# Window attention on 128 and 64 channels, with values projected once per pixel by way of DRAM

## The chip, the cores and the metric

The kernel runs on one core of a Trainium2 chip. TensorE (PE, with its weight loads as PEld), VectorE (DVE), ScalarE (ACT), GpSimd (POOL) and SyncE (SP) each work through their own list of instructions and meet at semaphores; DMAs are issued from SP and POOL. The metric is the device time of one execution in microseconds. Traces give every instruction its start and length, and the clock that TensorE was granted (1.00 is full speed).

## The reference

Input x is (4, 192, 64, 64) in float32: four images. Four layers follow each other: layer 0 (deformable convolution, attention over channels, MLP), layer 1 (attention of all 4096 pixels with each other), layer 2 (attention in overlapping windows, a high-frequency gate, a gated MLP), and layer 3 (a masked depthwise convolution whose taps depend on the image). The change lies in the first half of layer 2:

```python
y = _conv1x1(_ln_c(x, n1g, n1b), qkv_w, qkv_b)          # norm over 192 channels, then 576 outputs
cols = _unfold(y, WS, STRIDE, PAD)                      # windows of 8x8, every 6 pixels, padded by 3: 11x11
...
attn = jnp.einsum('blhic,blhjc->blhij', q, k)           # 6 heads of 32 channels, 64x64 scores per window
attn = attn + bias[None, None]
e = jnp.exp(attn - jnp.max(attn, axis=-1, keepdims=True))
s = jnp.sum(e, axis=-1, keepdims=True)
s_img = _reverse(s, H, W)                               # sums, folded back and added where windows overlap
o = jnp.einsum('blhij,blhjc->blhic', e, v)
o_img = _reverse(o, H, W).reshape(B, HEADS, ch, H, W)
out = (o_img / s_img[:, :, None]).reshape(B, C, H, W)
```

The padding is of y, so a window's q, k and v are zero outside the image, its scores there are the bias alone, and these enter the sums.

## The kernel before

The images run one after the other. `windows()` does the part above for one image, between layer 1 and `rest()`. It goes through 11 rows of windows (wr = 0..10); a row has three groups of four windows (g = 0..2, the last with three), a group two pairs. Everything inside is written in a fixed order by hand (`tc.manual_schedule()`, the loop from L1330 on), and each engine runs its instructions in that order.

**Layout.** The 192 channels lie as two halves of 96 partitions. A row of windows needs 8 rows of 64 pixels, of which the two upper ones are shared with the row before. `load` (L1077) brings the six new ones from DRAM with one DMA into xr; `norm_steps` (L1107) squares them on ACT (sq, L1112), takes means over the channels on PE (pv, L383), forms the reciprocal root on ACT and DVE (r, L400 to L402, L363, L364), spreads it back over the channels on PE (pb, L392) and multiplies on DVE into the padded tile xs (L1122). `shared` (L1131) copies the two shared rows of xs, qs and ks on POOL. xs has a 97th partition of ones, which carries the bias of the projection.

**Projections.** `project_rows` (L1142) makes q and k of the new rows, for each half two matmul pairs (L1150, L1151) of 384 columns, and ACT writes them to qs (L1154, with the temperature) and ks (L1156). [...]

**Scores.** `scores` (L1176): 24 matmuls of 32 channels for a group (L1185) into the only score tile s (three PSUM banks), then DVE adds the bias (L1191), takes the maximum (L1197) and subtracts it (L1198). `exponentials` (L1201): ACT's exp (L1203), then DVE's sums eh (L1205) and es (L1209).

**Outputs.** `turned` (L1216) projects the values of a pair of windows straight from xw (L1225, two matmuls with 128 pixels out and 192 channels), which ACT copies to vs (L1230), turns the exponentials by three transposes (L1233) and copies them into padded tiles et (L1237). `outputs` (L1243) multiplies values with exponentials (L1253) and adds up the sums per pixel (L1261) into the row's PSUM tile o. `collect` (L1266) copies o to ot (L1271, L1272), POOL adds the overlap with the row before (L1277); `inverses` (L1286) and `finish` (L1295: rb L1298, oi L1299) divide.

**Order.** Group n's transposes and outputs run while the scores of group n + 1 are brought to exponentials; outputs lag one pair behind. In group 0 `project_rows` for the next row stands in both pairs; in group 1 the next x is loaded, the row before is inverted and the norm for two rows on goes as far as its root; in group 2 that norm ends and the row before is finished. Once, after row 1, `load_image` (L2022) loads the whole image for `rest()` with 16 DMAs from SP. PSUM gives s three banks, o two, the norm one, and two banks take turns ("a") for projections, values, transposes and rb.

Of the kernel before, what the change touches and what calls it, by code (L numbers as in the profile page):

```python
# [10 lines left out]
F32 = mybir.dt.float32  # L11
# [58 lines left out]
_WIDE = ["l0_bfc2", "l2_projb", "l2_hftw", "l2_hftb", "l2_fc2b", "l3_bias", "l3_b2"]  # L70
# [11 lines left out]
def conv_seq_kernel(ctx: ExitStack, tc: tile.TileContext, a, out: bass.AP):  # L82
# [86 lines left out]
    for i in range(3):  # L169
# [4 lines left out]
        thetaT, phiT, gT, wW, qkvT, bias, v48, headsel, fc1_dram, fc1_bias, fc1b_dram, fc1b_bias, outb,  # L174
    ) = (None for _ in range(13))
# [10 lines left out]
    def constants():  # L186

        nonlocal thetaT, phiT, gT, wW, qkvT, bias, v48, headsel, fc1_dram, fc1_bias, fc1b_dram, fc1b_bias, outb
# [13 lines left out]
        qkvT = const([P + 1, 2, 3 * C], "qkvT")  # L202
        in_turn(nc.sync.dma_start(out=qkvT[:P], in_=a["qkvT"].rearrange("(k p) n -> p k n", p=P)))
        in_turn(nc.sync.dma_start(out=qkvT[P : P + 1, 1, :], in_=a["qkvb"]))
# [56 lines left out]
        with pool_of(name="foldq", bufs=1, space=PSUM) as pp:  # L261
            p = pp.tile([128, 2, 512], F32, tag="p", name="p_qkv")
            n = 3 * C // 2
            for u in range(2):
                for k in range(2):
                    nc.tensor.matmul(
                        p[P : P + 1, u, 0:n], lhsT=V["l2_n1b"][:, k], rhs=qkvT[:P, k, bass.ts(u, n)], start=k == 0, stop=k == 1
                    )
            row = qkvT[P : P + 1, 1, :].rearrange("p (u n) -> p u n", u=2)
            nc.vector.tensor_tensor(row, row, p[P : P + 1, :, 0:n], ALU.add)  # L270
            for k in range(2):
                nc.vector.tensor_scalar_mul(qkvT[:P, k, :], qkvT[:P, k, :], V["l2_n1g"][:, k])
            centred(qkvT[:P], pp)
# [72 lines left out]
    x_flat = [dram.tile([C, HW], F32, tag=f"xd{i}", name=f"xd{i}") for i in range(2)]  # L346
    xn_drams, x_drams = ([t.rearrange("(k p) n -> p k n", p=P) for t in ts] for ts in (xn_flat, x_flat))
# [712 lines left out]
    def windows(b, oi, load_image):  # L1060
# [3 lines left out]
        with ExitStack() as s:  # L1064
# [4 lines left out]
            given, norms, xws, qws = {}, {}, {}, {}  # L1069

            def new_rows(wr):

                top = STRIDE * wr - PAD
                r0, r1 = (PAD if wr == 0 else WS - STRIDE), min(WS, H - top)
                return r0, r1, top + r0

            def load(wr, by=nc.sync):  # L1077
                r0, r1, at = new_rows(wr)
                t = given[wr] = sb.tile([P, 2, 512], F32, tag="xr", name=f"xr_{b}_{wr}")[:, :, 0 : (r1 - r0) * W]
                by.dma_start(out=t, in_=x_drams[b % 2][:, :, at * W : (at + r1 - r0) * W])  # L1080
# [6 lines left out]
            for j in range(2):  # L1087
                xs = s1.tile([P + 1, 2, WS, SW], F32, tag=f"xs{j}", name=f"xs{j}_{b}")
                qs = s1.tile([P, 2, WS, SW], F32, tag=f"qs{j}", name=f"qs{j}_{b}")
                ks = s1.tile([P, 2, WS, SW], F32, tag=f"ks{j}", name=f"ks{j}_{b}")  # L1090
                for t in (xs, qs, ks):
                    nc.gpsimd.memset(t, 0.0)

                nc.gpsimd.memset(xs[P : P + 1, 1, (PAD if j == 0 else 0) : WS, inside], 1.0)
                sets.append((xs, qs, ks))
            ets = []
            for j in range(3):
                et = s1.tile([128, 3, 2, WS, WS + STRIDE], F32, tag=f"et{j}", name=f"et{j}_{b}")
                nc.gpsimd.memset(et, 0.0)
                ets.append(et)  # L1100
            rss = []
# [5 lines left out]
            def norm_steps(wr, src, dst, rows):  # L1107

                n, name = src.shape[2], f"l2n1_{b}_{wr}"
                q = n // 4  # L1110
                sq = s1.tile([P, 2, 512], F32, tag="ln_sq", name=f"sq_{name}", bufs=2)[:, :, :n]
                nc.scalar.activation(sq, src, AF.Square)  # L1112
                yield SQUARE
                pv = ps.tile([128, 512], F32, tag="n", name=f"pv_{name}")
                variances(pv[:, 0:q], src, mean192)
                variances(pv[:, 128 : 128 + q], sq, mean192)
                r = s1.tile([128, 128], F32, tag="ln_r", name=f"r_{name}", bufs=2)[:, 0:q]
                spread_variance(r, pv[:, 0:q], pv[:, 128 : 128 + q])
                yield from inverse_root_steps(r, r)
                pb = spread_quarters(r, n, P, ps, name).rearrange("p (r c) -> p r c", r=rows)  # L1120
                for k in range(2):
                    nc.vector.tensor_tensor(dst[:, k], src[:, k, :].rearrange("p (r c) -> p r c", r=rows), pb, ALU.mult)  # L1122

            def norm(wr, upto=None):

                r0, r1, _ = new_rows(wr)
                if wr not in norms:
                    norms[wr] = norm_steps(wr, given.pop(wr), sets[wr % 2][0][:P, :, r0:r1, inside], r1 - r0)
                links(norms[wr], upto)

            def shared(wr, i):  # L1131

                to, of = sets[wr % 2][i], sets[1 - wr % 2][i]
                r1 = new_rows(wr)[1]
                if i == 0 and wr == 2:
                    nc.gpsimd.memset(to[P : P + 1, 1, PAD - 1 : PAD, inside], 1.0)
                if wr > 0:
                    nc.gpsimd.tensor_copy(to[:, :, 0 : WS - STRIDE, :], of[:, :, STRIDE:WS, :])
                if r1 < WS:
                    nc.gpsimd.memset(to[:, :, r1:WS, :], 0.0)  # L1140

            def project_rows(wr, h):  # L1142
# [967 lines left out]
```

## Time and profile before

| | |
|---|---|
| median of three runs | 6396.97 us (6394.30, 6396.97, 6414.32) |
| the profiled execution's own time | 6392.29 us |
| its span (first to last instruction) | 6390.5 us |
| window stage of the four images | 268.7, 269.8, 269.0, 271.0 us |
| PE busy in these stretches | 246.7, 247.3, 246.5, 247.3 us |
| a steady row of windows | 23.05 us |
| mean granted clock over the span | 0.963 |

The page of the profile gives for the span the busy time of each engine; then the span in 40 slices; the DMA queues; the chain of work that ended last, by engine and by line; the costliest groups of instructions, with the mean length of one, the idle time of the engine before them and what ended it (its releaser); and the DMA issues. The same can be asked of the trace for a stretch of time, a line or a tile. PE's busy time is that of overlapping matmuls, so their pace is read from start to start rather than from the length of one.

### The profile page before, as it was taken

Reading aid. Unit: us, or ns where it says so; the run is one execution under the profiler, and the core shown is the slowest. Engines: PE = TensorE matmul, PEld = TensorE weight load, DVE = VectorE, ACT = ScalarE, POOL = GpSimd, SP = SyncE. Lnnn points to the kernel's source line nnn. Section 1 sums busy time; section 2 is a strip of 40 time slices with the busy share of each in tenths; the row PEclk is TensorE's granted clock in tenths of the full one; section 3 lists DMA queues with packets and bytes.
Section 4 is the critical chain, followed back from the end, with each engine's and each line's share of the span. In section 5 each row is a group of like instructions: output and inputs, shape, how many; then the busy total and the mean of one; then the engine's idle time right before and its main releaser. Section 6 shows DMA issues by size and latency. Waiting matters only on the chain.

```text
span 6390.5 us, 106371 instructions
## 1 busy us (share of the span) xinstructions
PE 5900.9 (92%) x40528; PEld 4039.0 (63%) x40528; DVE 4612.9 (72%) x6850; ACT 3779.2 (59%) x6552; POOL 2111.3 (33%) x2293
## 2 busy tenths in 40 slices
PE   7888999999989899999988899999998989999897
PEld 4455588886544568887654458888654457776543
DVE  3864199985677669996676839998567867765667
ACT  3764388875654358885654438887565536545542
POOL 2763077752200047772210017775220000003200
PEclk8989999999989999999999999999998999999998
DMA  6995267751010267772110057775111010001000
GB/s 193 308 316 152 81 195 223 224 178 37 24 29 17 74 200 221 226 222 69 35 36 24 21 145 227 222 223 171 36 27 29 21 57 11 13 15 38 5 7 22
DMA packets 330117, 698.60 MB, mean 109 GB/s; under 512 B 59894, under 2 KB 216838, under 8 KB 328839
## 3 DMA queue, kind: packets, MB, share of 16 engines
q0 software_dynamic: 92736, 455.22, 22.0%
q1 hardware_dynamic: 236038, 235.78, 13.5%
q8 instruction: 321, 5.26, 0.3%
q14 instruction: 190, 1.55, 0.1%
q10 hardware_dynamic: 832, 0.79, 0.0%
HBM read 611.25 MB, written 78.87 MB: 108 GB/s over the span
## 4 chain that ended last, share of the span: by engine, by line
PE 63%; DVE 20%; ACT 5%; DMA 5%; issue 4%; SPq 2%; POOL 1%; POOLq 0%; DVEq 0%; ACTq 0%
PE y L1041 11%; PE s L973 10%; PE h L650 7%; DVE ha L1403 2%; PE h L1595 2%; PE qk L1150 2%; PE v L1225 2%; PE o L878 2%; PE qk L1151 2%; DMA ring<-table,idx 2%; DVE ga L1403 2%; PE po L538 2%; DVE gate L1403 2%; DVE row L639 1%; DVE top L980 1%
## 5 line engine op out<-in xcount | busy, mean ns | idle before, releaser
L632 POOL DMA_INDIRECT ring<-table,idx x1152 | 1671.1, 1451 | 946.0 <-DVE row L639 172.7
L973 PE MATMUL s<-ths,ph 96*128 96x256 f32 x4096 | 982.5, 381 | 6.4 <-ACT sc L975 4.0
L973 PEld LDWEIGHTS s<-ths,ph 96*128 96x128 f32 x4096 | 776.6, 191 | 131.1 <-ACT sc L975 6.3
L638 ACT ACTIVATE row<-ring,pos 128x384 f32<-128x384 f32 x1152 | 673.0, 609 | 240.4 <-DVE xo L643 147.2
L639 DVE SCALAR_TENSOR_TENSOR row<-ring,fr,row 128x384 f32<-128x384 f32 x1152 | 673.1, 611 | 111.2 <-ACT row L638 106.3
L1041 PE MATMUL y<-sc,gx 128*97 128x256 f32 x3008 | 716.4, 379 | 0.0
L1041 PEld LDWEIGHTS y<-sc,gx 128*97 128x97 f32 x3008 | 489.3, 164 | 127.5 <-issue 5.1
L642 ACT ACTIVATE xo<-row,pos 128x192 f32<-128x192 f32 x1152 | 485.5, 448 | 64.2 <-PE h L650 32.2
L643 DVE SCALAR_TENSOR_TENSOR xo<-row,fr,xo 128x192 f32<-128x192 f32 x1152 | 445.4, 411 | 41.5 <-ACT xo L642 39.3
L975 ACT COPY sc<-s 128x1024 f32<-128x1024 f32 x376 | 377.1, 1003 | 157.0 <-PE s L973 154.2
L1038 DVE TENSOR_TENSOR sc<-sc,mbs 128x1024 f32<-128x1024 f32 x376 | 453.0, 1217 | 19.8 <-ACT mbs L999 19.7
L1039 ACT ACTIVATE sc<-sc 128x1024 f32<-128x1024 f32 x376 | 393.3, 1053 | 75.2 <-DVE sc L1038 72.1
L980 DVE TENSOR_TENSOR top<-top,sc 128x1024 f32<-128x1024 f32 x282 | 344.0, 1220 | 128.6 <-ACT sc L975 128.4
L650 PE MATMUL h<-ti,xo 128*128 128x192 f32 x2304 | 434.6, 327 | 0.0
L650 PEld LDWEIGHTS h<-ti,xo 128*128 128x128 f32 x2304 | 388.8, 190 | 28.8 <-issue 8.2
L1205 DVE TENSOR_REDUCE eh<-ex 128x12 f32<-128x768 f32 x132 | 125.4, 950 | 317.1 <-ACT ex L1203 317.1
L1403 DVE SCALAR_TENSOR_TENSOR ga<-gate,v,ga 128x1024 f32<-128x1024 f32 x234 | 300.3, 1283 | 6.7
L650 PE MATMUL h<-kept,xo 128*128 128x192 f32 x960 | 239.2, 381 | 70.5 <-DVE xo L643 62.0
L1645 POOL COPY gate<-gate 128x192 f32<-128x192 f32 x12 | 4.2, 348 | 904.9 <-ACT gate L1638 904.9
L650 PEld LDWEIGHTS h<-kept,xo 128*128 128x128 f32 x960 | 169.7, 210 | 162.9 <-DVE xo L643 116.4
L855 PE MATMUL h<-d_l0m,fc 128*128 128x256 f32 x768 | 217.5, 427 | 59.1 <-ACT z L1601 22.5
L1041 PE MATMUL y<-se,gx 128*97 128x256 f32 x1088 | 261.1, 380 | 0.5 <-ACT yn L1047 0.5
(402 smaller groups left out, 11090.8 us busy)
## 6 DMA issues: line engine op xcount, KB each, us to landing
ti<-table SPq DMA_DIRECT2D x768, 48.0 KB
ring<-table,idx POOLq DMA_INDIRECT x1152
xnd<-xn SPq DMA_DIRECT2D x4, 3270.0 KB
xi<-in_x_dram SPq DMA_DIRECT2D x32, 384.0 KB
xk<-xd SPq DMA_DIRECT2D x32, 384.0 KB
xd<-xc SPq DMA_DIRECT2D x64, 192.0 KB
table<-tt SPq DMA_DIRECT2D x32, 384.0 KB
xc<-xd SPq DMA_DIRECT2D x60, 192.0 KB
```

Source lines behind the costliest of these rows:

```text
L632: nc.gpsimd.indirect_dma_start(out=gt.rearrange("p q r c -> p (q r c)"), out_offset=None, in_=corners, in_offset=bass.IndirectOffsetOnAxis ...
L638: nc.scalar.activation(row, gt[:, 0], AF.Copy, scale=pos[:, t, 9 + tap : 10 + tap])
L639: nc.vector.scalar_tensor_tensor(row, gt[:, 1], fr[:, t, 9 + tap : 10 + tap], row, ALU.mult, ALU.add)
L642: nc.scalar.activation(xo[:, j, :], row[:, 0, :], AF.Copy, scale=pos[:, t, tap : tap + 1])
L643: nc.vector.scalar_tensor_tensor(xo[:, j, :], row[:, 1, :], fr[:, t, tap : tap + 1], xo[:, j, :], ALU.mult, ALU.add)
L650: nc.tensor.matmul(acc[m // 2][:, bass.ts(m % 2, C)], lhsT=xo.rearrange("p j c -> p (j c)")[:, bass.ts(m, 128)], rhs=tt, start=t == 0 and ...
L973: nc.tensor.matmul(p[:, t, :], lhsT=ph[:, bass.ts(G * g + t, 128)], rhs=ths[i], start=True, stop=True)
L980: nc.vector.tensor_tensor(tops[i], tops[i], to, ALU.max)
L1038: nc.vector.tensor_tensor(ex, ex, mbs[i].unsqueeze(1).to_broadcast([128, G, QN]), ALU.add)
L1039: nc.scalar.activation(ex, ex, AF.Exp)
L1041: nc.tensor.matmul(py, lhsT=gx[:, G * g + t, :], rhs=ex[:, t, :], start=g == 0 and t == 0, stop=g == NG - 1 and t == G - 1,)
L1403: nc.vector.scalar_tensor_tensor(acc[:, b], src(tap, b), w[:, tap : tap + 1], acc[:, b], ALU.mult, ALU.add)
```

## The change

Channels lie as 128 and 64 partitions (`M`, `Q`) instead of twice 96. Every row of windows takes a strip of six new rows (384 pixels, the last one fewer); the normed strip goes to its own tile xz without padding, and there is no ones row: biases of q and k come as a column (qkb) in ACT's eviction, the bias of the values (vb) in a DVE add. The six projection halves of 96 channels become three tiles of 128: t = 0 (q), t = 1 (k), t = 2 (the last 64 of both).

Values are computed once per pixel, three tiles of 128 pixels per row, written by two DMAs to a DRAM tensor with zero margins (zeroed once, by POOL's DMAs in image 0), and read back window by window by 16 DMAs (8 partitions each) into vw; xw, its POOL copies and the per-pair value matmuls are gone. Each group has one extra matmul of 384 columns (`keep_warm`) ahead of its first transposes. The order of the loop changes with it: t = 0 and t = 2 and the values in group 0, t = 1 in group 1; the sums of the exponentials behind the next group's bias, maximum and subtraction behind the sums (in group 0 behind the first values); the squares of the norm at the end of group 2.

In `constants()`, qkvT is folded with gamma and beta from raw tiles of 128 and 64 rows: the product of the raw weights with beta, which the ones row took before, goes into qkb and vb by ten small matmul groups, a matmul that spreads vb over 128 partitions, and some ten DVE instructions; it is loaded with three DMAs instead of two.

```diff
+            def strip(wr):
+                return (STRIDE if wr < NWIN - 1 else H - STRIDE * wr) * W, STRIDE * wr * W
+            def split(t, n):
+                return t[:, 0, 0:n], t[0:Q, 1, 0:n]
             def load(wr, by=nc.sync):
...
-                by.dma_start(out=t, in_=x_drams[b % 2][:, :, at * W : (at + r1 - r0) * W])
+                by.dma_start(out=lo, in_=x_flat[b % 2][0:M, at : at + n])
+                by.dma_start(out=hi, in_=x_flat[b % 2][M:C, at : at + n])
...
+            def project_rows(wr, t):
+                qs, ks = sets[wr % 2]
+                n = strip(wr)[0]
+                rows, chans = slice(PAD, PAD + n // W), bass.ts(t, M)
+                p = ps2.tile([128, 512], F32, tag="a", name=f"qk_{b}_{wr}_{t}")[:, :n]
+                for k, part in enumerate(split(xzs[wr], n)):
+                    nc.tensor.matmul(p, lhsT=qkvT[0 : part.shape[0], k, chans], rhs=part, start=k == 0, stop=k == 1)
...
+            def values(wr, part):
...
+                tiles = [i for i in (2 * part, 2 * part + 1) if 128 * i < n]
...
+                            nc.tensor.matmul(
+                                p[:, j, :], lhsT=of[:, bass.ts(i, 128)], rhs=qkvT[0 : of.shape[0], k, 2 * C :],
+                                start=k == 0, stop=k == 1,
+                            )
+                    nc.vector.tensor_tensor(
+                        vs[:, tiles[0] : tiles[-1] + 1, :], p, vb.unsqueeze(1).to_broadcast([128, len(tiles), C]), ALU.add
+                    )
+                if part == 0:
+                    return
...
+                for h in range(2):
+                    nc.sync.dma_start(out=to[h], in_=vs[half(h), 0:m, :])
+            def fetch(wr):
+                vw = vws[wr] = sb.tile([128, (NWIN + 1) // 2, C], F32, tag="vw", name=f"vw_{b}_{wr}")
+                for i in range(2):
+                    n = (NWIN + 1 - i) // 2
+                    for r in range(WS):
+                        row = values_dram[STRIDE * wr + r, STRIDE * i : STRIDE * i + 2 * STRIDE * n]
+                        at = 64 * i + WS * r
+                        nc.sync.dma_start(
+                            out=vw[at : at + WS, 0:n, :], in_=row.rearrange("(n c) k -> c n k", n=n)[0:WS]
+                        )
...
             def turned(wr, g, pair, given):
...
-                    nc.tensor.matmul(
-                        pv, lhsT=xw[: P + k, k, both, :].rearrange("p w j -> p (w j)"), rhs=qkvT[: P + k, k, 2 * C :],
-                        start=k == 0, stop=k == 1,
-                    )
-                v = sb.tile([128, C], F32, tag="v", name=f"vs_{b}_{wr}_{g}_{pair}", bufs=3)
-                nc.scalar.copy(v[rows], pv)
                 pt = ps2.tile([128, 512], F32, tag="a", name=f"t_{b}_{wr}_{g}_{pair}")
+                if pair == 0:
+                    keep_warm(pt[:, 0:384], 1)
```

The loop, with the start of the stage ahead of it:

```diff
-                shared(0, 0)
-                project_rows(0, 0)
-                norm(1, SQUARE)
-                project_rows(0, 1)
+                for t in range(3):
+                    project_rows(0, t)
+                    if t == 0:
+                        norm(1, SQUARE)
+                queries(0)
                 norm(1, VARIANCE)
-                queries(0)
-                inputs(0)
+                values(0, 0)
+                values(0, 1)
                 norm(1)
-                shared(1, 0)
+                fetch(0)
                 load(2)
-                ex = exponentials(0, 0, scores(0, 0))
+                ex, top = scores(0, 0)
+                lowered(0, 0, ex, top)
+                exponentials(0, 0, ex)
...
-                        if 0 < wr < NWIN - 2 and g == 0:
-                            norm(wr + 2, SQUARE)
                         if nxt[0] < NWIN:
-                            sc = scores(*nxt)
+                            sc, top = scores(*nxt)
+                        sums = summed(wr, g, ex)
+                        if nxt[0] < NWIN and (g > 0 or wr + 1 == NWIN):
+                            lowered(*nxt, sc, top)
...
-                            if g == 0 and wr + 1 < NWIN:
-                                project_rows(wr + 1, pair)
+                            if wr + 1 < NWIN:
+                                if g == 0:
+                                    project_rows(wr + 1, 2 * pair)
+                                    values(wr + 1, pair)
+                                if g == 1 and pair == 0:
+                                    project_rows(wr + 1, 1)
+                                if g == 0 and pair == 0:
+                                    lowered(*nxt, sc, top)
...
-                        if g == 0 and wr + 1 < NWIN:
-                            for i in (1, 2):
-                                shared(wr + 1, i)
-                            queries(wr + 1)
-                            inputs(wr + 1)
-                        if g == 2 and wr + 2 < NWIN:
-                            shared(wr + 2, 0)
+                        if wr + 3 < NWIN and g == 2:
+                            norm(wr + 3, SQUARE)
+                        if wr + 1 < NWIN:
+                            if g == 0:
+                                shared(wr + 1, 0)
+                                queries(wr + 1)
+                            if g == 1:
+                                shared(wr + 1, 1)
+                                fetch(wr + 1)
```

`lowered` is the maximum and its subtraction, `summed` the two sums, each taken out of `scores` and `exponentials`. The outputs take vw[wr] where they took vs.

## Prediction

> **What bounds the kernel now.** I read the page's engine and chain parts first, then tables of busy time by stretches in layer 2's window stage of image 0, then one steady row of it by groups and by the chain, last the issues of SP.
>
> ```profile
> PE 5900.9 (92%) x40528; PEld 4039.0 (63%) x40528; DVE 4612.9 (72%) x6850; ACT 3779.2 (59%) x6552; POOL 2111.3 (33%) x2293
> ...
> PE 63%; DVE 20%; ACT 5%; DMA 5%; issue 4%; SPq 2%; POOL 1%; POOLq 0%; DVEq 0%; ACTq 0%
> ```
>
> TensorE is busy for 92% and carries 63% of the chain. Apart from constants folded once, the change touches the window stage: 268.7, 269.8, 269.0 and 271.0 us in the four images, 1078.5 us or 17% of the span. Its rows (columns: stretch, length, busy PE, PEld, DVE, ACT, POOL, granted clock, DMA share, GB/s):
>
> ```profile
> 1494.79:1498.20 3.41, 1.78 (x73) 1.47 (x66) 0.79 (x3) 1.02 (x4) 3.26 (x11) 0.99 0.02 5
> 1498.20:1501.61 3.41, 2.31 (x74) 2.00 (x65) 3.34 (x5) 0.00 (x0) 0.00 (x0) 0.50 0.27 87
> ...
> 1508.43:1511.84 3.41, 3.41 (x30) 2.03 (x28) 0.00 (x0) 2.41 (x6) 0.00 (x0) 1.00 0.02 5
> 1594.00:1617.00 23.00, 21.20 (x342) 14.02 (x341) 14.48 (x22) 15.14 (x32) 6.64 (x17) 1.00 0.05 15
> ```
>
> A steady row of 11 windows takes 23.05 us (start of L1271 to the next), 21.2 of them PE at full clock; DVE and ACT have a third to spare. What TensorE does per row therefore sets the time, plus its one long wait. Groups of that row:
>
> ```profile
> L1225 PE MATMUL v<-qkvT,xw 96*128 96x192 f32 (+3 forms) x24 | 5.3, 342 | 0.0
> L1237 ACT COPY et<-t 64x384 f32<-64x384 f32 x11 | 5.3, 478 | 0.9 <-PE t L1233 0.8
> L1230 ACT COPY vs<-v 128x192 f32<-128x192 f32 (+1 forms) x6 | 1.9, 318 | 3.8 <-PE v L1225 3.8
> L392 PE MATMUL pb_l2n<-r_l2n,spread 128*96 128x96 f32 x8 | 0.9, 257 | 1.3 <-ACT r_l2n L364 1.3
> ```
>
> The last line is the wait: 1.3 us in group 2, until the norm's reciprocal root comes from ACT. Matmuls overlap, so I price by the paces of the chain:
>
> ```profile
> 1594.95 0.82 PE qk L1150 x2
> 1595.77 0.66 PE qk L1151 x2
> 1596.43 0.66 PE qk L1150 x2
> 1597.08 0.66 PE qk L1151 x2
> 1597.74 0.65 PE v L1225 x4
> ```
>
> One 384-column matmul (two records) costs 0.66, 0.82 where it is first; a pair of value matmuls (four records) 0.65.
>
> **The change, part by part.** Starts of scores (L1185) split a row into groups of 9.75, 4.78 and 8.52 us.
>
> *Values once per pixel.* Six pairs of value matmuls go (6 x 0.66 = 3.96 us of PE), three tiles of 128 pixels by two matmuls come (3 x 0.66 = 1.97). ACT loses six copies (1.9), POOL its copies of xs (six, 2.3), DVE gains the adds of the value bias (priced from L1198's 768 elements in 1.05: 0.55 and 0.35). *Projections* go from four to three per row: 5.5 to 3 x 1.37 = 4.1. *A warming matmul* of 384 columns per group is new: 3 x 0.66 to 0.82, taken as 0.72. The net on PE is -1.99 - 1.4 + 2.16 = -1.2 us per row.
>
> By group, with what follows on the other engines: group 0 loses two value pairs (1.32) and 5.5 of projection, gains 2.74 (t = 0, 2), 1.97 and 0.72: 9.75 - 1.4 = 8.35. Group 1: -1.32 + 1.37 + 0.72 = +0.77, so 5.55. Group 2: -1.32 + 0.72, two waits of value matmuls for evictions (about 0.5) go, and the long wait grows. Its length: behind the projection now in group 1 ACT does the k eviction (0.58), both inverses (1.04), two et copies (0.97) and r L400 (0.25), DVE L401 and L402 (0.47), ACT L363 and L364 (0.66); with some 0.05 for each hand-over that is 4.3 us, while PE has T 0.42, O 0.27, the variances 0.93 and the scores 0.73 = 2.35 to do. The wait is then **1.9 us** instead of 1.3: before, the chain to it ran over DVE (exp, eh, es, bias, max, sub), and moving the sums behind the bias clears that, but ACT is late next. Group 2 comes to 7.8. The row: 8.35 + 5.55 + 7.8 = **21.7 us**, 1.35 less.
>
> Costs put at nothing: sums, max and subtraction in another order (DVE 15.7 of 21.7, hidden under PE); squares at the end of group 2 (0.9 on ACT, a row ahead of need); two x loads for one; strips of 384 pixels. If DVE lost its cover, these would be worth up to 1 us per row.
>
> *The way through memory.* Per row SP issues 2 writes, 2 loads and 16 fetches, where it issued one load. The trace has no such fetch; the nearest rows of SP:
>
> ```profile
> L302 SPq DMA_DIRECT2D bias<-shifted x48: 685/685/812, 177.8 to 212.2; - x48
> ...
> L525 SPq DMA_DIRECT2D table<-tt x64: 574/635/3398, 400.4 to 3800.3; - x64
> ...
> L1080 SPq DMA_DIRECT2D xr<-xd x36: 304/305/328, 1490.3 to 5930.5; - x36
> ```
>
> Bounds per issue: 0.30 (contiguous x load) to 0.73 (L302's start to start, also to 8 partitions with two levels); I take 0.70, its shape being nearest. A load's last packet comes about 2.5 us after its issue (1568.68 to 1571.2), so I take 2.0 for the write and 1.4 for the last fetch. From written values to fetched windows: 2 x 0.65 + 2.0 + 16 x 0.70 + 1.4 = 15.9 us. In a steady row outputs need them 18.5 us after: hidden. The sum holds up to 0.86 us per issue; row 3, where the 16 loads of the image (L2027, L2028, 9.7 us) stand ahead in SP's queue, has no margin.
>
> In row 0 nothing hides it. The values are ready when the first scores start. The first outputs are wanted 8.3 us later (scores 0.80, bias, max, sub and exp 3.70, transposes 0.42, projection 1.37, values 1.40, transposes 0.42, hand-overs) and wait until 15.9, some 7.5 us. Also load(2) is queued behind fetch(0): SP reaches it at 1.3 + 2.0 + 11.2 = 14.5, it lands at some 17, and ACT, in order, stands at the squares of row 2 until then, with et copies, evictions and the next exponentials behind them (0.9 + 0.97 + 1.16), on which PE's projection, values and third scores wait in turn. From first to third scores that makes 20.2 us against 15.2 now (1497.71 to 1512.91): **+5.0** per image (+3.4 at 0.60 per issue, -1.6 at 0.32).
>
> *Clock.* The rows above show half the clock from 1498.20 to 1508.43, behind a stretch in which PE was busy for 1.78 of 3.41 us (0.52). The granted clock changes in steps of this length; cutting the whole trace into them, 0.53 busy divides those followed by a halving from the others, with 8 misplaced beside 60 halvings. Steady rows now have 0.60 at worst. A wait of 1.9 us inside one such step leaves 0.43. The step's phase is free; at least 1.6 us of the wait falls into one step in some 0.6 of the rows. A halved step takes up to 1.7 us, I take 1.0 net of PE's waits, and 0.4 of the rows, since the wait is only just long enough: 9 x 0.4 x 1.0 = **+3.6** per image (0 to +9). The wait for the first fetch adds some +1.5 beyond the opening half-clock spell that exists already.
>
> The Trainium skill, "TensorE: Matmul & The Clock Gate", Part 1, says that the half clock comes after at least one idle window of about 3.4 us. No step of a steady row is idle, so by the rule the 3.6 would fall away, 14 us over four images; the trace, which shows the halving behind 1.78 busy of 3.41, decides.
>
> *Once.* Constants are folded with more small instructions, woven into image 0's first layer, and POOL zeroes the pads (six issues at 0.68): POOL's memsets then end near 1495, and the queries near 1497.3, still ahead of the first scores at 1497.71. 0 to +3 us.
>
> **The sum.** Per image: nine rows x -1.35 = -12.1; row 0 +5.0; last row and tail -1.1 (no value matmuls left); clock +1.5 + 3.6. That is -3.1 per image, -12 for four. From the profiled execution, 6392.29 us (span 6390.5): 6380; the median of the runs shown is 4.7 above it: **6385**.
>
> **Rivals.**
> - *The clock falls in every row.* For it: 0.43 is clearly under 0.53. Against: the step's phase, and that a step with little more work in it stays above. Then +9 instead of +3.6: 2.3 us more per image than now, 6406, no change that counts.
> - *The fetch is cheap and the clock stays.* At 0.30 to 0.50 per issue row 0 costs -1.6 to +2, and without halvings an image gains 11 to 15: 6338 to 6351. For it: L1080's 0.305. Against: L302 and L525 are strided too, and at 0.63 to 0.69.
> - *Slower: SP can't deliver a row's windows in a row.* Above 0.86 us per issue (or with landings longer by 2.6) the fetch becomes the bound, row for row. At 0.90 rows take 22.8 and row 0 waits 11: with the outer costs an image is 16 us longer, +65: 6460. For it: 2.6 to 4.2 us at worst in L525 and L626, when the queue is held up, and row 3 without margin. Against: every median is under 0.70, and the stage moves 15 GB/s now.
> - *It doesn't do what it says.* "Spread over the groups": by the loop two of three projections and all values stay in group 0; group 1 alone gets one. If the sums behind the bias delay the outputs' es instead, each row loses up to 1.1 (0.95 + 0.2); PE's order gives them over 2 us, so I put this into the forecast's spread.
>
> **How the numbers follow.** A measurement of this kernel tells apart about 0.3%, 19 us: below 6378 is faster, above 6416 slower. Forecast 0.52, its own range 6367 to 6403 (0 to 0.6 of the rows halved, 0.60 to 0.73 per issue), of which 0.24 lies below 6378 and 0.28 within. Clock in every row 0.12 (0.02 slower). Cheap fetch 0.16, faster. Slow fetch 0.20, from 6416 to 6500. Faster 0.40, same 0.38, slower 0.22. For 8 in 10 the range reaches from 6345 (most of the cheap fetch) to 6440 (the nearer half of the slow one).
>
> **What would show it.** Right: rows of 21.7 with the clock at 1.00 and of 22.5 to 23 with some 0.5 in it; pb (L392 before) waiting for about 1.9 us on ACT; outputs of row 0 waiting 7 us on a DMA; SP's fetches 0.7 apart. Wrong: outputs of later rows waiting on vw (the slow fetch); rows at 21.7 throughout with clock 1.00 (no halvings, 6370 or less); PE waiting in group 0 for DVE's value adds or in group 1 for exponentials, which I hold to be hidden.

## The result, and the profile after

The changed kernel takes **6442.64 us** (median of five runs, 6441.41 to 6468.92) where the kernel before, in five runs beside it, takes 6396.97 (6394.30 to 6417.36): a ratio of **1.0072, interval [1.0045, 1.0099]**. It is slower by some 46 us; the forecast was 6385, and 6440 the upper end of its range. The profiled execution is the slowest of the five, 6468.92 us with a span of 6467.1; a second profile of the same kernel, taken with the experiments (`as_changed`), has a span of 6445.4. Where the two differ is said below.

The page of the changed kernel, engines and chain of waits:

```profile
PE 5977.0 (92%) x40124; PEld 4009.8 (62%) x40124; DVE 4633.4 (72%) x6943; ACT 3723.1 (58%) x6332; POOL 1980.6 (31%) x1980
...
PE 65%; DVE 18%; ACT 6%; DMA 5%; issue 4%; SPq 1%; POOL 0%; DVEq 0%; ACTq 0%; POOLq 0%
```

PE has 404 instructions fewer than before and is busy for 76 us more. The change was to take work from PE; by this line the work that is left keeps it busy for longer.

One steady row, from the start of scores (now L1273) to the next, in the table of busy time by stretches (columns: stretch, length, busy PE, PEld, DVE, ACT, POOL with instructions, granted clock, DMA share, GB/s):

```profile
1660.50:1684.06 23.56, 22.00 (x332) 12.65 (x331) 14.77 (x24) 13.83 (x27) 3.94 (x10) 1.00 0.21 57
```

23.56 us at full clock with PE busy for 22.00; it was 23.05 with 21.2, and 21.7 was forecast. By groups the row was 9.75 / 4.78 / 8.52, the forecast said 8.35 / 5.55 / 7.8, and it is 9.94 / 6.15 / 7.47. The last group is about as expected; the two groups that hold projections and values are 1.6 and 0.6 longer. The chain of waits shows which steps (columns: start, us, engine, step, line, instructions):

```profile
1672.63 1.68 PE qk L1197 x4
1674.31 2.08 PE v L1225 x8
1676.39 0.48 PE t L1321 x3
...
1677.31 1.68 PE qk L1197 x4
1678.99 1.04 PE v L1225 x4
```

A projection takes 1.68, not 1.37; a tile of values 1.04, not 0.66. The groups of the same row, with the wait:

```profile
L1225 PE MATMUL v<-qkvT,xz_l2n 128*128 128x192 f32 (+1 forms) x12 | 3.3, 376 | 0.0
L424 PE MATMUL pb_l2n<-r_l2n,spread 128*128 128x96 f32 x8 | 1.1, 284 | 1.5 <-ACT r_l2n L396 1.5
L1229 DVE TENSOR_TENSOR vs<-v,vb 128x384 f32<-128x384 f32 (+1 forms) x2 | 0.9, 457 | 4.8 <-PE v L1225 4.8
```

The long wait stands where it was expected, on ACT's root ahead of pb (L424, which was L392), 1.5 us long and not 1.9. The value adds on DVE wait for PE, and PE never for them.

What every projection does can be read from the single records of PE. Each fp32 matmul is two weight loads (LDW) and two passes (MM); start in us, and rows in use:

```
changed, L1197             before, L1150 and L1151
1672.559 LDW 128           1594.876 LDW 96
1672.560 MM  128           1594.878 MM  96
1672.667 LDW 128           1594.958 LDW 96
1672.987 MM  128           1595.284 MM  96
1673.401 LDW  64           1595.285 LDW 97
1673.403 MM   64           1595.609 MM  97
1673.510 LDW  64           1595.611 LDW 97
1673.830 MM   64           1595.939 MM  97
1674.240 LDW 128           1595.941 LDW 96
```

Before, the weights of the next matmul are loaded as soon as a pass has started (1595.285 behind 1595.284), and passes follow at 0.325. In the changed kernel the load with another number of rows comes only when the last pass is over: 0.414 behind its start, and the pass after the load takes 0.427 to the next one. That is 0.19 us for each change between 128 and 64 rows, and every product over the channels now has two. The Trainium skill, "TensorEngine Tiling (Array Packing)", Key Properties, says: "Changing tiling mode (not just tile) drains the TensorE". The records agree if 64 and 128 rows count as two modes and 96 and 97 as one; the page gives no price, the runs give 0.19.

The whole difference of the profiled spans, 76.6 us, by place and beside the terms of the forecast (us over four images):

```
                                                   forecast   measured
nine rows per image (-1.35 / +0.51 each)              -48.6      +18
halved steps of the clock in later rows               +14        +23
first three groups, with the opening half clock       +26        +22
row 1, last two rows and the tail                      -4        -18
prologue, end of layer 1 to the first scores            0        +13
image 0 ahead of its window stage                    0 to +3     +18
sum                                                   -12        +76
```

The first line is a steady row's difference times nine (36 in all); the second counts the changed kernel's halved steps alone, and the kernel before has two, worth 4 us, which the fourth line holds; the fourth is what the stretch from first to last scores (943.6 before, 995.2 after) leaves, and 6 us at the last collects. The last line is no firm number: the first scores of image 0 start at 1519.5 in this profile and at 1514.5 in the second one. In the second profile the clock's opening spell is missing in three images of four, and first to last scores sum to 975.0; the steady row is the same to 0.01.

### The profile page after: what moved, and what is told of

Its sections match the earlier page's. It is cut to its first block, busy times and chain, and to the rows that moved or that the text cites. A ratio compares the mean times of both kernels' runs of the same rounds, so it can differ in the third digit from the quotient of the medians.

```text
span 6467.1 us, 105953 instructions
## 1 busy us (share of the span) xinstructions
PE 5977.0 (92%) x40124; PEld 4009.8 (62%) x40124; DVE 4633.4 (72%) x6943; ACT 3723.1 (58%) x6332; POOL 1980.6 (31%) x1980
## 4 chain that ended last, share of the span: by engine, by line
PE 65%; DVE 18%; ACT 6%; DMA 5%; issue 4%; SPq 1%; POOL 0%; DVEq 0%; ACTq 0%; POOLq 0%
PE y L1073 11%; PE s L1005 10%; PE h L682 6%; PE qk L1197 3%; DVE ha L1503 2%; PE v L1225 2%; PE h L1695 2%; DMA ring<-table,idx 2%; PE o L910 2%; DVE ga L1503 2%; PE po L570 2%; PE t L785 2%; DVE gate L1503 1%; DVE row L671 1%; DVE top L1012 1%
## 5 line engine op out<-in xcount | busy, mean ns | idle before, releaser
L1325 ACT COPY et<-t 64x384 f32<-64x384 f32 x484 | 231.9, 479 | 293.2 <-PE t L1321 288.7
```

## The experiments

The first four kernels below ran on a chip where the kernel before takes 6531.35 us, since layer 0's gathers are slower there (the 241st starts at 508 us in before_64_rows, at 468 in the first profile of the kernel before); the others on two chips where it takes 6394.8 to 6397.4. Ratios are against the kernel before on the same chip.

**rows128: no change of rows.** The second part of the channels takes 128 rows: channels 64 to 191, with zero weights for the 64 that the first part has already.

```diff
-                return t[:, 0, 0:n], t[0:Q, 1, 0:n]
+                return t[:, 0, 0:n], t[:, 1, 0:n]
...
-by.dma_start(out=hi, in_=x_flat[b % 2][M:C, at : at + n])
+by.dma_start(out=hi, in_=x_flat[b % 2][Q:C, at : at + n])
...
-in_turn(nc.sync.dma_start(out=raw[0:Q, 1], in_=a["qkvT"][M:C]))
+in_turn(nc.sync.dma_start(out=raw[Q:M, 1], in_=a["qkvT"][M:C]))
+nc.gpsimd.memset(qkvT[0:Q, 1, :], 0.0)
```

> The changed kernel, but the second part of the channels also takes 128 rows of TensorE (it is loaded with channels 64 to 191, and the weights of the doubled channels 64 to 127 are zero), so that no matmul of projection, values and norm has 64 rows. Theory (a change between 128 and 64 rows empties TensorE, some 0.19 us each): four records of a projection take 1.31 us instead of 1.68, a pixel tile of values 0.66 instead of 1.04, the variances 0.95 instead of 1.25; a row falls from 23.56 to about 21.5, the first scores come some 2.5 us sooner in each image, the whole is 80 to 100 us below the changed kernel, 6345 to 6365, less what halvings of the clock take back (up to 30). Rival (weights of 128 columns are slower whatever their rows): paces and rows stay, 6440.

Measured: 6518.88 against 6531.35, 0.9968 [0.9947, 0.9989]. Rows at full clock are 8.23 / 5.51 / 8.05 = 21.79, the forecast's 8.35 / 5.55 / 7.8 = 21.7 almost exactly. About five rows of eight have a group 2 of 9.63 to 9.66 instead. Three steps of the clock around such a wait (columns as above):

```profile
1687.73:1691.14 3.41, 1.34 (x61) 1.07 (x52) 1.33 (x3) 2.76 (x7) 0.00 (x0) 1.00 0.32 87
1691.14:1694.55 3.41, 3.41 (x21) 2.37 (x23) 3.04 (x5) 0.42 (x2) 0.00 (x0) 0.50 0.21 53
1694.55:1697.96 3.41, 3.35 (x79) 1.86 (x72) 1.67 (x4) 2.61 (x6) 0.00 (x0) 1.00 0.02 5
```

A step in which PE is busy for 1.34 of 3.41 us is followed by one at half clock. The groups name the wait:

```profile
L425 PE MATMUL pb_l2n<-r_l2n,spread 128*128 128x96 f32 x8 | 1.2, 294 | 2.1 <-ACT r_l2n L397 2.1
```

With PE's products cheaper, PE is at pb sooner than ACT's root: the wait grew from 1.5 to 2.1. What follows: the emptying costs 1.77 us of each row, and behind it stands the forecast's own next bound.

**before_64_rows: the price put into the kernel before.** The second half of q and k takes 64 of its 97 rows, so 32 channels and the bias are left out.

```diff
-nc.tensor.matmul(p, lhsT=qkvT[:, 1, chans], rhs=xs[:, 1, rows, inside], start=False, stop=True)
+nc.tensor.matmul(p, lhsT=qkvT[0:Q, 1, chans], rhs=xs[0:Q, 1, rows, inside], start=False, stop=True)
```

> The kernel before, but the second matmul of each q and k projection takes only 64 of its 97 rows; it leaves out 32 channels and the bias of q and k. Theory (changing rows empties TensorE): the four projections of a row alternate between 96 and 64 rows, 8 changes of 0.19 us, so groups 0 are 1.5 us longer (9.75 to 11.2), a row 24.5, 60 us in all, about 6455. Rival (128 columns are slow): 96 columns as before, nothing changes, 6397.

One run: 6602.45, 71 above the median of the kernel before. The chain of waits in group 0:

```profile
1703.52 0.82 PE qk L1150 x2
1704.34 0.82 PE qk L1151 x2
1705.16 0.82 PE qk L1150 x2
1705.98 0.82 PE qk L1151 x2
```

Every matmul now takes the 0.82 that only the first took before, and half of them multiply a third fewer rows. Group 0 went from 9.75 to 10.73, 0.98 for its changes between 96 and 64 rows, 0.12 to 0.17 each; 1.5 for all of them was expected. Nothing else was touched, so the cost is in the change of rows, not in 128 rows or in the new order. It also showed what I had not expected: the half clock at the start of each stage lasts 24 to 27 us instead of 7 to 10.

**early_weights: the constants of image 0.** The weights are loaded at the top of the constants, in the new order of columns, and scaled in place.

```diff
+        for rows, k, src in ((slice(0, M), 0, a["qkvT"][0:M]), (slice(0, Q), 1, a["qkvT"][M:C])):
+            for c, of in ((0, 0), (M, C), (2 * M, M), (2 * M + Q, C + M)):
+                n = M if c < 2 * M else Q
+                in_turn(nc.sync.dma_start(out=qkvT[rows, k, c : c + n], in_=src[:, of : of + n]))
+            in_turn(nc.sync.dma_start(out=qkvT[rows, k, 2 * C :], in_=src[:, 2 * C :]))
...
-            in_turn(nc.sync.dma_start(out=raw[:, 0], in_=a["qkvT"][0:M]))
-            in_turn(nc.sync.dma_start(out=raw[0:Q, 1], in_=a["qkvT"][M:C]))
...
-                to, of = qkvT[rows, k], raw[rows, k]
...
+                nc.vector.tensor_scalar_mul(qkvT[rows, k], qkvT[rows, k], gamma[rows, k])
```

> The changed kernel, but the 192 x 576 weights are loaded at the top of the constants, already in the new order of columns, and are scaled in place there. Theory (the 18 us that image 0 loses ahead of the windows are waits of VectorE and TensorE, in order, for weights that are loaded only where they are used): the wait of 6.4 us goes and with it most of the rest, 10 to 16 us less than the changed kernel, about 6428. Rival (the small matmuls and vector instructions themselves displace the gather): 0 to 4 us less.

The reason to try it is in the timeline of the changed kernel, DVE and POOL, while layer 0 of image 0 gathers (columns: start, us, engine, line, operation; in brackets the idle time before and its releaser):

```profile
174.78 0.55 DVE L293 TENSOR_SCALAR qkvT<-w_qkv,wide 128x256 f32<-128x256 f32 x2 [6.44 <-DMA w_qkv<-in_qkvT_dram]
185.98 0.16 DVE L278 COPY qkb<-p_qkb 128x3 f32<-128x3 f32 x1 [6.39 <-PE p_qkb L277]
```

```profile
188.07 0.96 POOL L664 DMA_INDIRECT ring<-table,idx  x1 [7.59 <-DVE row L671]
```

DVE stands behind the load and behind the products with beta for 6.4 us each, and the next gather on POOL, which wants a row from DVE, stands for 7.6. From the start of the 31st gather to that of the 49th the changed kernel takes 39.4 us, the kernel before 26.3. (The expectations speak of gathers 60 to 96: these are POOL's records, of which a gather has two, a wait and an issue, so that it is this stretch of 18 gathers.) Measured: 6595.73, 1.0093 [1.0067, 1.0118], no gain. The 18 gathers take 34.8 where rows128 and no_warm take 38.4 on this chip, and the 30 ahead of them 46.2 where those two take 45: of the 10 to 16 us expected, 2 are there.

**no_warm: without the warming matmul.**

```diff
-                if pair == 0:
-                    keep_warm(pt[:, 0:384], 1)
```

> The changed kernel without the warming matmul of each group. Theory (TensorE sets the row, the clock follows its busy share): each group is 0.7 us shorter at full clock, a row 21.4, but more stretches fall under half busy, which costs 1 us in two rows of three: 40 to 70 us less than the changed kernel. Rival (the warming matmul pays for itself): halvings in every row, within 10 us of the changed kernel or above it.

Measured: 6586.87, 1.0087 [1.0060, 1.0113], between the 1.0072 and 1.0103 that the changed kernel has. Rows are 9.25 / 5.87 / 6.82 at full clock, 1.6 shorter, but some five of eight have a group 2 of 8.3 to 8.4. From first to last scores three images take 237.3 and one 240.8, where early_weights, which has the matmul, takes 241 to 251 on the same chip. The rows won less than the 2.1 expected, since group 1 gives only 0.28, and the halved steps took some of it back. As long as the wait is there, the warming matmul pays back part of its price, but by this stretch not all of it.

**as_changed: the changed kernel again**, beside the next three.

> The changed kernel itself, for a second profile beside the kernel before on one chip. Rows of 9.94 + 6.15 + 7.47 us as in its first profile, first scores some 20 us later in image 0; 1.005 to 1.012 of the kernel before.

6456.39 against 6395.81, 1.0103 [1.0085, 1.0121], the rows as before. This chip puts it 14 us higher than the first comparison; both intervals say slower.

**rows128_inv: rows128 and ACT's queue.** `inverses` of the row before, 1.04 us of ACT ahead of the norm's root, goes behind the exponentials of group 1.

```diff
-                            if wr > 0 and g == 1 and pair == 0:
-                                inverses(wr - 1)
...
                             ex = exponentials(*nxt, sc)
+                        if wr > 0 and g == 1:
+                            inverses(wr - 1)
```

> The variant with 128 rows in both channel parts, and the two inversions (Ln, Exp) of group 1 moved behind its exponentials, so that ACT reaches the norm's root 1.04 us sooner. Theory (the wait of some 1.9 us before the spreading matmuls halves the clock in over half of the rows): the wait falls to about 0.9, group 2 to 7.0 and no halving follows in steady rows (now 9.65 in two rows of three): a row 20.8 to 21.0 throughout, against the variant without the move 60 to 80 us less, 0.985 of the kernel before. Rival (the halvings have another cause): group 2 falls by 1.0 but halvings stay, 35 us less.

6301.77, **0.9855 [0.9837, 0.9874]**, as expected. A row and a stretch of one step's length around the wait, and the wait itself:

```profile
1600.00:1620.61 20.61, 19.66 (x339) 13.29 (x330) 14.79 (x24) 13.80 (x28) 3.94 (x12) 1.00 0.23 62
...
1608.00:1611.41 3.41, 2.51 (x59) 1.97 (x44) 2.57 (x6) 2.55 (x6) 0.00 (x0) 1.00 0.37 109
```

```profile
L425 PE MATMUL pb_l2n<-r_l2n,spread 128*128 128x96 f32 x8 | 1.1, 284 | 0.9 <-ACT r_l2n L397 0.9
```

The row is 8.23 / 5.50 / 6.88 = 20.61; the wait went from 2.1 to 0.9, by the 1.04 that was moved and a little more, and no steady row is halved: the least busy step of the clock in these rows has 0.70. The chain of waits shows the products that the forecast had priced:

```profile
1617.22 1.49 PE qk L1197 x4
1618.71 1.30 PE v L1225 x8
1620.01 0.33 PE t L1321 x3
...
1620.77 1.49 PE qk L1197 x4
1622.26 0.65 PE v L1225 x4
```

Values take 0.65 a tile (1.04 before the padding). A projection has 1.49 here, but the chain cuts its pieces at the modelled ends of matmuls; from start to start it takes 1.39 (1.68 before the padding, 1.37 in the forecast), and the transposes behind the values 0.42 (0.48).

**rows128_inv_loads: the constants once more**, with the loads put behind the first folded weight's and in place.

```diff
+        def weights():
+            for rows, k, src in ((slice(0, M), 0, a["qkvT"][0:M]), (slice(Q, M), 1, a["qkvT"][M:C])):
+                both = src[:, 0 : 2 * C].rearrange("p (u n) -> p u n", u=2)
+                for cols, part in ((slice(0, 2 * M), both[:, :, 0:M]), (slice(2 * M, 2 * C), both[:, :, M:C])):
+                    in_turn(nc.sync.dma_start(out=qkvT[rows, k, cols].rearrange("p (u n) -> p u n", u=2), in_=part))
...
+        fc1_dram, fc1_bias = folded("fc1", V["l0_g2"], V["l0_b2"], V["l0_bfc1"], weights)
```

> As the variant before it, and the weights of q, k and v are loaded in the new column order right behind the load of the first folded weights, where SP has nothing to do, and are scaled in place. Theory (image 0 loses its time to waits for these loads and the chain of instructions at one place): the section of gathers 60 to 96 falls from 38 to about 27 us with no new wait ahead of it; 10 us less than the variant without. Rival (the small instructions displace the gather wherever they stand): within 4 us of it.

6306.11, 0.9864 [0.9847, 0.9881], no different from rows128_inv, as its rival had it. The 18 gathers take 27.7 us instead of 37.7, and the 30 ahead of them 47.8 instead of 43.4.

**rows128_inv_no_warm: and the warming matmul out.** The diffs of rows128_inv and no_warm together.

> 128 rows, inversions moved, and no warming matmuls. Theory (with the long wait gone TensorE sets the row and the clock stays): 3 x 0.7 us less per row, 18.9 to 19.5, 60 us less than with them. Rival (ACT and DVE, 14 to 15.7 us per row, now set the waits, and TensorE's share falls under half): a gain under 1 us per row or halvings in every row, no better than with them.

```profile
1600.00:1619.50 19.50, 17.77 (x325) 12.21 (x324) 14.70 (x23) 13.80 (x28) 3.94 (x10) 1.00 0.26 66
```

6276.48, **0.9817 [0.9802, 0.9832]**, less than both kernels. The row is 7.54 / 5.50 / 6.47 = 19.50. With the wait at 0.9 the three warming matmuls cost 1.1 of a row and save nothing in it; in group 1 the one matmul costs nothing, since PE waits there anyway, 0.73 us for ACT's exponentials (L1294).

**changed_inv and before_inv: the same move without the padding**, in the changed kernel and in the kernel before.

> The changed kernel with only the inversions moved behind the exponentials of group 1, with 128 and 64 rows as it was. Theory (two causes that add up: emptying of TensorE, and the wait in group 2 with its halvings): group 2 falls from 7.47 by 0.9 to 1.0 and has no halvings, groups 0 and 1 stay at 9.94 and 6.15, a row 22.6; the whole some 45 us under the changed kernel, 1.002 to 1.005 of the kernel before. Rival (without the emptying there would be no gain, the norm is just as late): 7.47 stays.

> The kernel before, with only the inversions moved behind the exponentials of group 1. Theory (its wait of 1.3 us in group 2 hangs on DVE's chain, not on ACT): rows stay at 23.05 within 0.1, the whole within 0.1% of the kernel before. Rival (ACT's order is late there too): group 2 falls by up to 1 us, 40 us less.

changed_inv: 6413.23, 1.0026 [1.0014, 1.0038], rows 9.94 / 6.15 / 6.87 with no halved steps among the steady ones. before_inv: 6401.98, 1.0011 [1.0001, 1.0021], rows 9.74 / 4.77 / 8.50. The wait in the groups of changed_inv, then of before_inv:

```profile
L424 PE MATMUL pb_l2n<-r_l2n,spread 128*128 128x96 f32 x8 | 1.1, 284 | 0.9 <-ACT r_l2n L396 0.9
```

```profile
L392 PE MATMUL pb_l2n<-r_l2n,spread 128*96 128x96 f32 x8 | 0.9, 257 | 1.3 <-ACT r_l2n L364 1.3
```

In the kernel before the wait stays at 1.3 though ACT has 1.04 less ahead of it: there ACT itself waits, for DVE, 0.98 us in before_inv where it waited 0.57:

```profile
1621.35 0.37 ACT L363 ACTIVATE r_l2n<-r_l2n,eps 128x96 f32<-128x96 f32 x1 [0.98 <-DVE r_l2n L402]
```

In the changed kernel it falls from 1.5 to 0.9. So the sums behind the bias did clear DVE's chain, and ACT's own queue is what was late next, as the forecast had it.

**sums_at_once: rows128_inv with the sums straight behind their exponentials again.**

```diff
-                        sums = summed(wr, g, ex)
+                        sums = sums_next
...
                             ex = exponentials(*nxt, sc)
+                            sums_next = summed(*nxt, ex)
```

> The variant with 128 rows and the inversions moved, but with the sums of the exponentials right behind each exponential again, ahead of the next group's bias. Theory (what the move of the sums buys is DVE's 1.2 us ahead of the bias, and in group 0 alone DVE's chain of sums, bias, value adds, maximum and subtraction is late for the next exponential): group 0 goes from 8.23 to about 8.9, groups 1 and 2 stay, a row 21.3, 25 to 30 us more than without. Rival (DVE has cover everywhere): rows stay at 20.6.

6331.72, 0.9901 [0.9885, 0.9918]. Group 0 takes 8.50 instead of 8.23 (8.66 in early rows), the others are as they were; first to last scores 213.0 to 214.3 instead of 209.7 to 211.1. The timeline of PE in that group:

```profile
1650.11 0.91 PE L786 MATMUL t<-spread,ident 128*128 128x384 f32 x2 [0.21 <-DVE oi L1387]
```

PE's first work behind the scores waits for DVE's oi, which stands behind the sums. The order is worth 0.27 to 0.5 of a row, less than the 0.7 expected. That makes 3.3 us an image, 13 of the 28 between the two profiled spans (the kernels ran on different chips); 12 more lie ahead of the first scores of image 0, where nothing was changed.

**no_products, best_no_products: without the products with beta** (qkb and vb zero) in rows128_inv and in rows128_inv_no_warm; **best_again** is the latter unchanged, beside it.

```diff
-            p = pp.tile([128, 512], F32, tag="p", name="p_qkb")
...
-                    nc.tensor.matmul(
-                        p[to, at : at + 1], lhsT=raw[rows, k, cols], rhs=beta[rows, k], start=k == 0, stop=False,
-                    )
...
-            nc.tensor.matmul(p[:, 256 : 256 + C], lhsT=ones[0:1, :], rhs=row[:, 2 * C :], start=True, stop=True)
-            nc.vector.tensor_copy(vb, p[:, 256 : 256 + C])
+            nc.vector.memset(qkb, 0.0)
+            nc.vector.memset(vb, 0.0)
```

> The variant with 128 rows and the inversions moved, without the small matmuls and vector instructions that make the bias columns qkb and vb in the constants; it leaves out the products of the weights with beta and the given biases (zeros stand in their place). Theory (their chain, in order on TensorE and DVE, holds up the gather at one place): the section of gathers 60 to 96 falls from 38 us to about 30, and the first scores of image 0 come 6 to 10 us sooner. Rival (the wait for the late load alone holds it up, or the loss turns up elsewhere): the first scores come at the same time within 4 us.

> The fastest variant so far (128 rows, inversions moved, no warming matmuls) once more, as the one beside which the next is judged: rows of 7.54 + 5.50 + 6.47 us, 0.980 to 0.984 of the kernel before.

> The same without the small matmuls and vector instructions that make qkb and vb; it leaves out the products with beta and the given biases (zeros stand in their place). Theory (the loss in image 0 is that chain): the section of gathers 60 to 96 is 10 us shorter, and so is the whole, 0.0015 less in the ratio to the kernel before. Rival (what is gained there is lost again before the window stage, as in the earlier profiles): the section is shorter, the whole the same within 4 us.

no_products 6326.07, 0.9880 [0.9857, 0.9904], above rows128_inv though it does less. best_again 6283.34, 0.9825 [0.9810, 0.9841]; best_no_products 6272.85, 0.9804 [0.9785, 0.9822]. The two medians are 10.5 us apart, as the theory had it, but the intervals overlap. The 18 gathers fall from 38.9 to 29.4 us without the products, but by the 241st gather only 2.8 of that is left, and the first scores of image 0 start later, at 1518.7 against 1514.2. With the same constants they start anywhere from 1509 to 1531 in these profiles, and the kernel before_inv starts them at 1511.8 where the kernel before has 1497.7. So the 13 us of the section are shown, and that the products make most of them (9.5); that the products cost the whole kernel 13 us is not. What decides image 0's start stays open, and with it how much of the 18 us ahead of its window stage is the change's.

## Why the prediction was wrong

**The step that failed:** "Matmuls overlap, so I price by the paces of the chain". The paces, 0.66 for a matmul of 384 columns and 0.65 for a pair of value matmuls, are those of 96 and 97 rows, between which PE loses nothing. The diff shows 128 and 64 rows side by side, and I took the paces over without asking whether anything in the trace has two such neighbours. Per row:

```
                     forecast   measured   difference
three projections      4.1        5.04       +0.9
three value tiles      1.97       3.12       +1.15
variances              0.93       1.34       +0.4
pb, 128 for 96 columns 0.75       0.96       +0.2
the wait               1.9        1.5        -0.4
```

Together +2.3 beside +1.86 in the row's time (23.56 for 21.7). rows128 takes the changes of rows out and gets 21.79: the order, the covers and the engine that is late next were right, and the sum to 0.1. That closeness is partly luck, for errors cancel: group 0 came out 0.12 under the forecast and group 2 0.25 over it. By the prediction's own terms group 2 adds up to 8.0 (8.52 - 1.32 + 0.72 - 0.5 + 0.6), not 7.8, and the value pairs that go were priced at 0.66, where five of the six in that row of the kernel before have 0.68 to 0.79 from start to start. In four images this step is 67 us of the 89 between forecast and profile.

**Values and projections fewer:** right in count, and worth 1.3 us a row as forecast, once they are of one row count.

**The wait moves from DVE to ACT:** right (changed_inv against before_inv). Its 1.9 us was 1.5 because the longer variances on PE fill part of it; in rows128 it is 2.1.

**Halved steps:** in rows128 right in kind, by the mark of 0.53 busy that the forecast had read from the trace: the 21 halvings in its later rows come behind steps of 0.37 to 0.53, and in rows128_inv, with no step under 0.70, there are none. There they hit about 0.6 of the rows, the first estimate, which was cut to 0.4 without a row to say so, and cost 1.6 each, not 1.0. In the changed kernel 12 rows of 40 have them, and the mark doesn't hold: all 12 come behind steps in which PE's records fill 0.54 to 0.66 (the one ahead of the half clock at 1592.5 has 1.91 of 3.41 us), so that by the mark none would have come. The rule that the forecast set against its row, a half clock behind at least one idle window (the Trainium skill, "TensorE: Matmul & The Clock Gate", Part 1), would have none of these either; the runs decide against it.

**The fetch:** wrong in size, and row 0 wrong in cause. SP's issues by line (line, queue, operation, count, then the shortest, median and longest ns of one, first and last start):

```profile
L1237 SPq DMA_DIRECT2D values<-vs x88: 580/611/1829, 1518.9 to 6062.3; - x88
...
L1247 SPq DMA_DIRECT2D vw<-values x704: 264/302/1307, 1520.4 to 6068.6; - x176
```

0.302 us in the records, and 6.06 us for the 16 of row 0 (0.38 each), not 0.70: the row that looked like it (L302, eight partitions too) was the wrong one, and the plain x load with 0.305 the right one. In image 0 fetch(0) was issued by 1526.4 and the first outputs came at 1532.6; in the whole kernel outputs waited for a fetch once, in row 0 of image 3, for 0.68 us, not for 7.5 in each image. The rival of the slow fetch, the only one on the slow side, named a time near the measured one with a mechanism that no run shows. Row 0 did get longer, from 15.2, 14.4, 15.1, 14.7 to 18.9, 18.9, 18.9, 14.1 between first and third scores, by the clock:

```profile
1519.50:1524.20 4.70, 2.42 (x99) 1.60 (x98) 4.54 (x6) 0.72 (x1) 0.00 (x0) 1.00 0.48 120
1524.16:1541.20 17.04, 16.82 (x94) 8.48 (x95) 5.58 (x9) 5.70 (x11) 3.02 (x8) 0.50 0.18 47
```

Behind a stretch with PE busy for half the time come 17 us at half clock. In the second profile three images have no such spell, and there row 0 takes 12.6, 12.8 and 13.7, 1.0 to 2.6 less than before. That is near the "-1.6 at 0.32" that the forecast gave for a cheap fetch, but not a proof of it: the kernel before has a spell of half clock (10.2 us) in these rows, and they have none.

**Put at nothing:** the prologue of each image has three projections and the values of row 0 ahead of the first scores, 3.2 us of value matmuls alone, and it went from 18.2 to 21.3 and more. I followed the loop and not the lines ahead of it. The constants (0 to +3) hold up 18 gathers by 13 us; how much of that reaches the whole is open.

**The sum** of what was right would have been the cheap side: rows128 alone, with the constants and the prologue in it, is at 0.9968. None of the rivals held the emptying, so the range missed as well, by 2.6 us.

## What to carry to other kernels

Before you price a matmul by a pace, look whether its neighbours in that row of the trace have the same number of rows; if a change brings 128 next to 64, fill the short part up with real data and zero weights, which costs PE no time: here a ratio of 1.007 to 1.010 became 0.997. Then look at the longest wait of the bounding engine, find which queue is late at it, and move from ahead of it what nobody wants yet: that gave as much again (0.997 became 0.986), because the wait of 2.1 us also halved the clock behind it in 21 of 32 rows. A guard against the half clock (the warming matmuls) has to be measured: here it paid back part of its price while the wait was there, and nothing once the wait was short.

## What the runs showed of the hardware

- A half clock can outlast its cause. At the start of the window stage it never lasts over 10.2 us in the kernels with one row count (96 with 97, or 128). Where rows change between 128 (or 96) and 64, it is missing in 8 of 24 images, lasts 3.4 to 10.2 us in 3 and 13.7 to 37.6 in 13, though PE's records fill 98% of such a time (16.82 of 17.04 above). An emptied PE seems not to count as busy; that would also fit the 12 halvings behind steps of 0.54 to 0.66. It is an inference, no run measured it.
- Going from 96 to 97 rows and back costs nothing (0.325 from pass to pass), from 96 to 64 it costs 0.12 to 0.17, from 128 to 64 0.19.
- Eight records of pb with 96 columns take 0.96 us with 128 weight columns and 0.75 with 96. Their weight loads start 0.112 us apart in the one and 0.085 in the other, and the passes follow at the same pace: at this length the load sets it.
- A DMA of 8 partitions from DRAM is issued in 0.30 us, a write of 64 partitions in 0.61.
